# Shared expert in units of 256 rows, its first layer split around its second; B turned by four transposes

## The chip, the cores and the metric

The kernel runs on one core of one Trainium2 chip. A core has PE (matrix products, with its weight loads), DVE (vector), ACT (scalar functions and copies), POOL (general) and SP (which here issues most transfers). Each engine works through its own list of instructions in order, and waits where an operand or a buffer is not there yet. The metric is the device time of one launch in microseconds (us); lower is better.

## The reference, cut to what matters

Four sequences of 1024 tokens with 256 channels go through a Mamba block, a layer norm, a mixture of experts and a second layer norm.

```python
# Mamba block: 512 inner channels, 16 states
h = rms_norm(x) @ w_in                         # 256 -> 1024, split into xs and res
xs = silu(causal_conv4(xs)); res = silu(res)
delta_low, B, C = split(xs @ w_xproj, [16, 32])
delta = softplus(delta_low @ w_dt + b_dt)
state[l] = exp(delta * A) * state[l-1] + delta * xs * B[l]    # per channel and state
y = sum_n(state * C);  x = layernorm(x + x + ((y + xs * D) * res) @ w_out)
# mixture of experts: 8 routed experts, 2 for each token, and one shared by all
normed = rms_norm(x)
shared = relu(normed @ sw1 + sb1) @ sw2 + sb2                 # 256 -> 1024 -> 256
w, idx = top2(sigmoid(normed @ router_w.T)), weights normalised
routed = sum over the 2 chosen e of w_e * (relu(normed @ ew1[e] + eb1[e]) @ ew2[e] + eb2[e])
x = layernorm(x + shared + routed)
```

All of it is in float32.

## The kernel before

**Chunks and scan.** The 4096 tokens are 8 chunks of 512, two for each sequence. A chunk's scan has 16 steps, one for each state `n`. A step handles four blocks of 128 channels: ACT makes `da` (an exponential of 128x512, L515), DVE runs the recurrence (L518), multiplies by the row of C (L531) and, for the next step, multiplies `xs` by the row of B (L451). POOL does the fourth block of that product (L456) and adds each step's result into `y` (L532). The rows of B and C are spread over partitions by small products on PE, `pb` (L437). In the first chunk, steps from 3 on get their input from PE instead, by products with a diagonal matrix (`diagonal`, `products`), which need B with tokens on partitions: `B_T`.

**Front.** `front` makes the inputs of a chunk's scan. Its projection `pp` (L360) holds the low rank of delta, then B, B and C in quads of 32 partitions. In the first chunk B with tokens on partitions is computed a second time at this place, by 16 products (`B_T`, L368) that take blocks of `xs` as weights. ACT copies 16 rows of `pp` into `proj` (L377), and `pz` (L393) makes delta of it; softplus follows with an exponential, a logarithm `y<-y` (L417), an add on POOL (`delta`, L421), and ACT then starts `y` with `xs * D` (L424). The first chunk's front runs alone; the others run beside the scan of the chunk before.

**Experts.** `tail` finishes a chunk: output projection, layer norm, routing, and the scatter of token rows to the lists of their experts (POOL, L707). It also leaves `x1T`, the normed rows with channels on partitions, and `combT`. The work of the experts is then a list of units of 128 rows: for each chunk 4 units of the shared expert and, in the chunks' order, 1, 11, 8, 8, 8, 8, 8 and 16 routed blocks. `up` is a unit's first layer: two halves of eight products `pu` of 128 columns each in one PSUM buffer of the pool `ps_up` (two buffers), and four evictions by ACT with bias and ReLU into a buffer `h` of 128x4x128 (L911). `down` is the second layer: eight products of 256 columns into `pd` (pool `ps_dn`, one buffer). For the shared expert a ninth adds the biases (L939), and ACT copies `pd` into one half of `rs` (pool `one`, a single buffer, L947); after every second unit POOL issues a transfer that adds `rs` to `sums` in memory (L952). For routed blocks ACT scales into `rb` and an indirect transfer adds it (L964).

`moe` orders a unit: weights ahead (`need`), the first layer of the next unit, the transposes of the rows of the unit after that (`rows_T`, `pbt`), then the second layer of this unit, then the rows of later blocks (`load_rows`). Each `yield` is one step. Weights of the first and of the second layer have two buffers each; all shared units of a chunk use one load.

**What sets the order.** The loop over scan steps calls `other_work` four times a step, which owes 0.85 of an expert step each time. On top of that a planner in the framework orders each engine's list when the kernel is built, by its own estimate of when operands are ready; buffers of a pool are handed out in the order of the program's text. After the last scan the rest of the expert units run with the last chunk's `tail`, and `finish` normalises and writes the output.

Of the kernel before, what the change touches and what calls it, by code (L numbers as in the profile page):

```python
# [8 lines left out]
F32 = mybir.dt.float32  # L9
# [4 lines left out]
P = 128  # L14
# [28 lines left out]
BS = P  # L43
TOKENS = NSEQ * SEQ
# [26 lines left out]
def mamba_moe_kernel(  # L71
# [189 lines left out]
    def front(b, c):  # L261
# [101 lines left out]
        if alone:  # L363

            pt = ps_up.tile([P, TC // P, N], F32, tag="up", name="B_T")
            for t in range(TC // P):
                for k in range(KB):
                    nc.tensor.matmul(  # L368
                        pt[:, t, :], lhsT=xs[:, k, t * P : (t + 1) * P], rhs=w_xp_sb[:, k, QUAD : QUAD + N],
                        start=(k == 0), stop=(k == KB - 1),  # L370
                    )
            by_token.append(pt)
# [3 lines left out]
        proj = one.tile([R, TC], F32, tag="proj", name=f"proj_{s}")  # L376
        nc.scalar.copy(proj, pp[0:R, :])  # L377
# [85 lines left out]
    def turned():  # L463

        xs, TT = scans[chunks[0]][0], LEN[chunks[0]] // P
        pt = by_token.pop()
        B_T = const.tile([P, TT, N], F32, tag="B_T", name="B_T_sb")
        nc.scalar.copy(B_T, pt)
        x_T = two.tile([P, TT, DI], F32, tag="w2", name="x_T")
        by_token.extend((x_T, B_T))  # L470
        for k in range(KB):
            pt = ps_up.tile([P, TT, P], F32, tag="up", name=f"x_T_{k}")
            for t in range(TT):
                nc.tensor.transpose(pt[:, t, :], xs[:, k, t * P : (t + 1) * P], ident)
            nc.scalar.copy(x_T[:, :, k * P : (k + 1) * P], pt)
            if k % 2:
                yield
# [65 lines left out]
    def tail(b, c):  # L543
# [52 lines left out]
        shared_left.extend(range(TC // BS))  # L596
# [203 lines left out]
    for b, c in chunks:  # L800
        units += [(b, c, SHARED, j) for j in range(LEN[b, c] // BS)]
        units += [(b, c, None, j) for j in range(BLOCKS[b, c])]
# [65 lines left out]
    def rows_T(u):  # L868
# [4 lines left out]
        if e is not None:  # L873
            rows_in[u] = channels[b, c][0][:, :, j * BS : (j + 1) * BS]
            return
# [15 lines left out]

    def up(u, hidden):
# [3 lines left out]
        wb = held[key(u)]["b"]  # L896
        for h in range(2):
# [24 lines left out]
    shared_rows, pending = {}, []  # L922

    def down(u, hidden):
# [3 lines left out]
        for h in range(2):  # L928
            for i in range(half):
# [3 lines left out]
                    start=(m == 0), stop=(m == HB - 1 and e is None),  # L933
# [3 lines left out]
        if e is not None:  # L937

            nc.tensor.matmul(  # L939
                pd, lhsT=channels[b, c][1][:, j * BS : (j + 1) * BS], rhs=b2_sb,  # L940
                start=False, stop=True,
            )
            shared_left.pop()
            if j % 2 == 0:
                shared_rows[b, c] = one.tile([P, 2, D], F32, tag="rs", name=f"rs_{u}")
            rs = shared_rows[b, c]
            nc.scalar.copy(rs[:, j % 2, :], pd)  # L947
            if j % 2:
                first = P + b * SEQ + FIRST[b, c] + (j - 1) * BS

                def add():
                    nc.gpsimd.dma_start(  # L952
                        sums_of[first : first + 2 * BS, :].rearrange("(t p) d -> p t d", p=P),
                        rs, accum_op=ALU.add,
                    )

                pending.append(add)
            return
# [13 lines left out]
    def moe():  # L972

        hidden = {}
        for u in range(last):
# [8 lines left out]
            for v in range(u + 1, u + 3):  # L984
                need(v, "w1")
            if u + 1 < last and ready(u + 1):
                hidden[u + 1] = []
                for _ in up(u + 1, hidden[u + 1]):
                    yield True
            evict_all()  # L990
            need(u + 3, "w1")
# [5 lines left out]
            for _ in down(u, hidden.pop(u)):  # L997
                yield True
# [209 lines left out]
```

## Time and profile before

| | |
|---|---|
| time, median of 3 runs | 1596.62 us (1595.63 to 1603.1) |
| the profiled execution: time; span of its instructions | 1597.39 us; 1595.7 us |
| busy: PE, DVE, POOL, ACT | 1256.2, 1279.3, 1140.0, 1065.6 us |
| `da` exponentials on ACT, 512 | 353.0 us, 697 ns each |
| recurrences on DVE after `da`, idle before them for `da` | 47.7 us in 22 places |
| first layer of shared units: 1024 PE instructions | 133.2 us busy |
| evictions of all first layers on ACT, 800 | 229.2 us, 368 ns each |
| `rs` copies on ACT, 32 | 11.8 us, 369 ns each; 14.7 us of waiting for the add in 4 places |
| `B_T` products, 32 PE instructions | 6.5 us busy |

A line of the page or of an answer gives source line, engine and operation, then output and inputs by the program's names. In lists in order of time the first two numbers are the start and the duration in us, and the bracket is the idle time before and what ended it. PE counts a float32 product as two instructions. Busy shares are means over stages with different limits.

### The profile page before, as it was taken

The numbers are of one execution on the slowest core, as the hardware profiler recorded it, in microseconds if no ns is written. First come the engines' busy times: TensorE is split into PE (matmuls) and PEld (weight loads), VectorE is DVE, ScalarE is ACT, GpSimd is POOL, SyncE is SP. The second block draws the span as 40 slices with busy tenths as digits, with TensorE's granted clock in tenths as the row PEclk, the third lists the DMA queues.
The fourth block names the chain that finished last, engine by engine and source line by source line (L and its number), as shares of the span: only waits on it lengthen the run. The fifth ranks groups of instructions, "written<-read, shape, count | busy, mean of one in ns | idle before, by whom it ended". The sixth has DMA issues, their size and how long they took to land. (4 is left out here: it accounts for less than half of the span.)

```text
span 1595.7 us, 20861 instructions
## 1 busy us (share of the span) xinstructions
PE 1256.2 (79%) x6667; PEld 971.3 (61%) x6667; DVE 1279.3 (80%) x1422; ACT 1065.6 (67%) x2345; POOL 1140.0 (71%) x886
## 2 busy tenths in 40 slices
PE   6588366874678798979798879888779978999990
PEld 3356233652356666667567756776567767889980
DVE  3899899989997798989998999999989889320005
ACT  4757557775778567877788778766786757434442
POOL 2378975898678876898689978987799787431123
PEclk8699777977789999999998999899999999999995
DMA  4000000441016552475246633564167448559986
GB/s 121 1 0 1 26 14 14 149 116 20 13 61 182 173 173 77 141 213 179 54 123 194 194 85 121 171 185 106 51 191 208 129 126 248 166 160 323 308 269 218
DMA packets 160276, 211.65 MB, mean 133 GB/s; under 512 B 20617, under 2 KB 138130, under 8 KB 160162
## 3 DMA queue, kind: packets, MB, share of 16 engines
q1 hardware_dynamic: 135954, 181.75, 35.1%
q0 software_dynamic: 17216, 21.57, 7.6%
q10 hardware_dynamic: 6992, 6.95, 1.3%
q8 instruction: 55, 0.90, 0.2%
q14 instruction: 59, 0.48, 0.1%
HBM read 178.97 MB, written 31.27 MB: 132 GB/s over the span
## 5 line engine op out<-in xcount | busy, mean ns | idle before, releaser
L532 POOL TENSOR_TENSOR y<-y,hs 128x2048 f32<-128x2048 f32 x128 | 595.8, 4655 | 82.1 <-DVE hs L531 81.7
L515 ACT ACTIVATE da<-delta,chan_sb 128x512 f32<-128x512 f32 x512 | 353.0, 697 | 196.6 <-DVE hs L518 191.6
L931 PE MATMUL pd<-w,h 128*128 128x256 f32 x1600 | 390.6, 389 | 24.6 <-ACT h L911 11.3
L931 PEld LDWEIGHTS pd<-w,h 128*128 128x128 f32 x1600 | 301.8, 195 | 95.1 <-issue 20.0
L518 DVE TENSOR_TENSOR_SCAN hs<-da,state,hs 128x512 f32<-128x512 f32 x256 | 317.8, 1270 | 27.8 <-ACT da L515 26.7
L902 PEld LDWEIGHTS pu<-xT,w 128*128 128x128 f32 x2176 | 275.5, 203 | 61.2 <-ACT xT L885 42.1
L902 PE MATMUL pu<-xT,w 128*128 128x128 f32 x2176 | 280.3, 287 | 28.2 <-ACT xT L885 28.2
L531 DVE TENSOR_TENSOR hs<-hs,pb 128x2048 f32<-128x2048 f32 x128 | 290.8, 2272 | 2.3 <-ACT state L526 0.8
L911 ACT ACTIVATE h<-pu,wb 128x128 f32<-128x128 f32 x800 | 229.2, 368 | 69.8 <-PE pu L902 65.5
L518 DVE TENSOR_TENSOR_SCAN hs<-da,hs 128x512 f32<-128x512 f32 x204 | 240.9, 1209 | 20.9 <-ACT da L515 20.5
L456 POOL TENSOR_TENSOR hs<-xs,b 128x512 f32<-128x512 f32 x118 | 169.4, 1439 | 68.0 <-ACT b L449 49.1
L451 DVE TENSOR_TENSOR hs<-xs,pb 128x1536 f32<-128x1536 f32 (+1 forms) x115 | 198.0, 1722 | 13.3 <-ACT b L449 7.7
L964 POOL DMA_INDIRECT sums<-rb,xb x68 | 107.9, 1587 | 133.3 <-ACT rb L961 33.5
L293 PE MATMUL pi<-hT,w_in_sb 128*128 128x512 f32 x256 | 142.8, 683 | 32.8 <-DVE xs L325 12.3
L437 PE MATMUL pb<-parts,pick 128*128 128x512 bf16 x243 | 97.3, 403 | 76.0 <-DVE hs L451 26.0
L219 DVE BATCH_NORM_STATS2 bnst_l<-o 128x6 f32<-128x256 f32 x32 | 11.9, 410 | 156.2 <-DMA o<-sums 156.2
L902 PEld LDWEIGHTS pu<-x1T,w 128*128 128x128 f32 x1024 | 127.8, 199 | 14.3 <-issue 10.3
L902 PE MATMUL pu<-x1T,w 128*128 128x128 f32 x1024 | 133.2, 285 | 0.0
L293 PEld LDWEIGHTS pi<-hT,w_in_sb 128*128 128x128 f32 x256 | 50.4, 214 | 98.4 <-issue 34.8
L564 PE MATMUL po<-w_out_sb,y 128*128 128x256 f32 x256 | 68.7, 429 | 34.7 <-POOL y L554 28.7
L564 PEld LDWEIGHTS po<-w_out_sb,y 128*128 128x128 f32 x256 | 54.4, 218 | 54.0 <-POOL y L554 35.7
L707 POOL DMA_INDIRECT rows<-hn,to x64 | 63.2, 987 | 33.0 <-issue 15.8
(198 smaller groups left out, 1562.0 us busy)
## 6 DMA issues: line engine op xcount, KB each, us to landing
w<-in_ew SPq DMA_DIRECT2D x136, 1024.0 KB
w<-in_sw SPq DMA_DIRECT2D x16, 1024.0 KB
xb<-rows SPq DMA_DIRECT2D x68, 129.0 KB
x<-in_x SPq DMA_DIRECT2D x8, 512.0 KB
sums<-summed ACTq DMA_DIRECT2D x8, 512.0 KB
sums<-rs POOLq DMA_DIRECT2D x16, 256.0 KB
o<-sums SPq DMA_DIRECT2D x3, 1024.0 KB
out<-o ACTq DMA_DIRECT2D x3, 640.0 KB
```

Of the source, the lines that this page charges most:

```text
L293: nc.tensor.matmul(pi, lhsT=w_in_sb[:, k, m * P : (m + 1) * P], rhs=hT[:, k, :], start=(k == 0), stop=(k == KD - 1),)
L451: nc.vector.tensor_tensor(hs[:, 0:on_pool, :], xs[:, 0:on_pool, :], pb.unsqueeze(1).to_broadcast([P, on_pool, TC]), ALU.mult,)
L456: nc.gpsimd.tensor_tensor(hs[:, k, :], xs[:, k, :], copy, ALU.mult)
L515: nc.scalar.activation(da, delta[:, k, :], AF.Exp, scale=chan_sb[:, k, CA + n : CA + n + 1])
L518: nc.vector.tensor_tensor_scan(hs[:, k, :], da, scaled_inputs.pop(0) if by_pe(step) else hs[:, k, :], 0.0 if c == 0 else state[:, k, n : n ...
L531: nc.vector.tensor_tensor(hs, hs, pb.unsqueeze(1).to_broadcast([P, KB, LEN[b, c]]), ALU.mult)
L532: nc.gpsimd.tensor_tensor(y, y, hs, ALU.add)
L564: ins = nc.tensor.matmul(po[:, i, :], lhsT=y[:, k, t * P : (t + 1) * P], rhs=w_out_sb[:, k, :], start=(k == 0), stop=(k == KB - 1),)
L902: nc.tensor.matmul(pu[:, i, :], lhsT=w[:, k, at : at + P], rhs=xT[:, k, :], start=(k == 0), stop=(k == KD - 1),)
L911: nc.scalar.activation(t[:, i, :], pu[:, i, :], AF.Relu, bias=wb[:, m : m + 1])
L931: nc.tensor.matmul(pd, lhsT=hidden[h][:, i, :], rhs=w[:, m, :], start=(m == 0), stop=(m == HB - 1 and e is None),)
L964: nc.gpsimd.indirect_dma_start(sums_of[:, :], bass.IndirectOffsetOnAxis(xb[:, TOKEN : TOKEN + 1].bitcast(U32), 0), rb, None, compute_op=AL ...
```

## The change

`front` no longer computes B a second time. It copies 64 rows of `pp` in place of 16 for the first chunk, and `turned` makes `B_T` by four transposes of that copy.

The shared expert works in units of 256 rows, two for each chunk. Its first layer is made in quarters: `quarter` issues four products of 256 columns into one PSUM buffer, and two evictions of 128x256. `up` does two quarters of such a unit; `down_shared` does the second layer in four quarters, with the third and fourth quarter of its own first layer after its first two, and the two first steps of the next unit's `up` ahead of its last two. `pd` is 128x2x256, and one copy moves it to `rs`. In `moe` the weights after next are asked for inside `down_shared`. `down` keeps the routed part alone. Routed units are otherwise as before.

```diff
+PAIR = 2 * BS
@@ front @@
-        if alone:
-            pt = ps_up.tile([P, TC // P, N], F32, tag="up", name="B_T")
-            for t in range(TC // P):
-                for k in range(KB):
-                    nc.tensor.matmul(
-                        pt[:, t, :], lhsT=xs[:, k, t * P : (t + 1) * P], rhs=w_xp_sb[:, k, QUAD : QUAD + N],
-                        start=(k == 0), stop=(k == KB - 1),
-                    )
-            by_token.append(pt)
...
-        proj = one.tile([R, TC], F32, tag="proj", name=f"proj_{s}")
-        nc.scalar.copy(proj, pp[0:R, :])
+        low_rank = one.tile([2 * QUAD if alone else R, TC], F32, tag="proj", name=f"proj_{s}")
+        nc.scalar.copy(low_rank, pp[0 : low_rank.shape[0], :])
+        proj = low_rank[0:R, :]
+        if alone:
+            by_token.append(low_rank)
@@ turned @@
+        pt = ps_up.tile([P, TT, 2 * QUAD], F32, tag="up", name="low_rank_T")
+        for t in range(TT):
+            nc.tensor.transpose(
+                pt[:, t, :], low_rank[:, t * P : (t + 1) * P], ident[0 : 2 * QUAD, 0 : 2 * QUAD]
+            )
...
-        nc.scalar.copy(B_T, pt)
+        nc.scalar.copy(B_T, pt[:, :, QUAD : QUAD + N])
@@ tail @@
-        shared_left.extend(range(TC // BS))
+        shared_left.extend(range(TC // PAIR))
@@ units, rows_T @@
-        units += [(b, c, SHARED, j) for j in range(LEN[b, c] // BS)]
+        units += [(b, c, SHARED, j) for j in range(LEN[b, c] // PAIR)]
...
-            rows_in[u] = channels[b, c][0][:, :, j * BS : (j + 1) * BS]
+            rows_in[u] = channels[b, c][0][:, :, j * PAIR : (j + 1) * PAIR]
+    def quarter(u, q, xT, hidden):
+        w, wb = held[key(u)]["w1"], held[key(u)]["b"]
+        pu = ps_up.tile([P, 2, PAIR], F32, tag="up", name=f"pu_{u}_{q}")
+        for i in range(2):
+            for k in range(KD):
+                at = (2 * q + i) * P
+                nc.tensor.matmul(
+                    pu[:, i, :], lhsT=w[:, k, at : at + P], rhs=xT[:, k, :],
+                    start=(k == 0), stop=(k == KD - 1),
+                )
+        def evict():
+            t = hid.tile([P, 2, PAIR], F32, tag="h", name=f"h_{u}_{q}")
+            for i in range(2):
+                m = 2 * q + i
+                nc.scalar.activation(t[:, i, :], pu[:, i, :], AF.Relu, bias=wb[:, m : m + 1])
+            hidden.append(t)
+        evictions.append(evict)
@@ up @@
+        if units[u][2] is not None:
+            for q in range(2):
+                quarter(u, q, xT, hidden)
+                yield
+                evict_all()
+            hidden.append(xT)
+            return
+    def down_shared(u, hidden, ahead):
+        b, c, e, j = units[u]
+        w, xT = need(u, "w2"), hidden.pop()
+        pd = ps_dn.tile([P, 2, D], F32, tag="dn", name=f"pd_{u}")
+        for q in range(4):
+            if q >= 2:
+                next(ahead, None)
+                yield
+                evict_all()
+            for i in range(2):
+                m = 2 * q + i
+                for t in range(2):
+                    nc.tensor.matmul(
+                        pd[:, t, :], lhsT=hidden[q][:, i, t * P : (t + 1) * P], rhs=w[:, m, :],
+                        start=(m == t == 0), stop=False,
+                    )
+            if q == 3:
+                for t in range(2):
+                    at = j * PAIR + t * P
+                    nc.tensor.matmul(
+                        pd[:, t, :], lhsT=channels[b, c][1][:, at : at + P], rhs=b2_sb,
+                        start=False, stop=(t == 1),
+                    )
+            yield
+            evict_all()
+            if q < 2:
+                quarter(u, q + 2, xT, hidden)
+                yield
+                evict_all()
+            if q == 1:
+                need(u + 2, "w1")
+        for _ in ahead:
+            pass
+        shared_left.pop()
+        rs = one.tile([P, 2, D], F32, tag="rs", name=f"rs_{u}")
+        nc.scalar.copy(rs, pd)
...
@@ moe @@
-            for v in range(u + 1, u + 3):
-                need(v, "w1")
+            routed = units[u][2] is None
+            need(u + 1, "w1")
+            if routed:
+                need(u + 2, "w1")
+            ahead = iter(())
             if u + 1 < last and ready(u + 1):
                 hidden[u + 1] = []
-                for _ in up(u + 1, hidden[u + 1]):
+                ahead = up(u + 1, hidden[u + 1])
+            if routed:
+                for _ in ahead:
                     yield True
-            evict_all()
-            need(u + 3, "w1")
+                evict_all()
+                need(u + 3, "w1")
...
-            for _ in down(u, hidden.pop(u)):
+            of = hidden.pop(u)
+            for _ in down(u, of) if routed else down_shared(u, of, ahead):
                 yield True
```

More of the change, by code (lines that the diff above doesn't have):

```diff
@@ L465, in turned @@
         xs, TT = scans[chunks[0]][0], LEN[chunks[0]] // P
-        pt = by_token.pop()
+        low_rank = by_token.pop()
+        pt = ps_up.tile([P, TT, 2 * QUAD], F32, tag="up", name="low_rank_T")
[3 more added lines that the diff above has]
+            )
         B_T = const.tile([P, TT, N], F32, tag="B_T", name="B_T_sb")
-        nc.scalar.copy(B_T, pt)
+        nc.scalar.copy(B_T, pt[:, :, QUAD : QUAD + N])
         x_T = two.tile([P, TT, DI], F32, tag="w2", name="x_T")
@@ L920, in evict_all, with add @@
             evictions.pop(0)()
-    shared_rows, pending = {}, []
+    pending = []
+    def down_shared(u, hidden, ahead):
[34 more added lines that the diff above has]
+        nc.scalar.copy(rs, pd)
+        first = P + b * SEQ + FIRST[b, c] + j * PAIR
+        def add():
+            nc.gpsimd.dma_start(
+                sums_of[first : first + PAIR, :].rearrange("(t p) d -> p t d", p=P),
+                rs, accum_op=ALU.add,
+            )
+        pending.append(add)
     def down(u, hidden):
@@ L932, in down @@
                     pd, lhsT=hidden[h][:, i, :], rhs=w[:, m, :],
-                    start=(m == 0), stop=(m == HB - 1 and e is None),
+                    start=(m == 0), stop=(m == HB - 1),
                 )
@@ L936, in down @@
             evict_all()
[L937 to L958, printed above, removed]
         xb = blocks_in.pop(u)
```

## The prediction

> **What bounds the kernel now.** I read three things, in this order: the share of busy time by stage, the waits of the engine that is nearest to full, and the stretches in which that engine does nothing. The first view is the busy time of each engine in chosen stretches (columns after the bounds: length, then busy us of PE, weight load, DVE, ACT, POOL; then the granted clock, the DMA share and GB/s).
>
> ```profile
> 40.00:80.00 40.00, 22.18 (x75) 12.99 (x73) 35.84 (x41) 30.84 (x48) 15.23 (x9) 0.62 0.00 1
> ...
> 800.00:1200.00 400.00, 338.51 (x1813) 261.86 (x1814) 377.82 (x393) 312.33 (x695) 342.60 (x228) 0.95 0.48 142
> ...
> 1440.00:1480.00 40.00, 40.00 (x274) 37.14 (x274) 0.00 (x0) 16.83 (x56) 7.49 (x5) 1.00 1.01 321
> ```
>
> So there are three stages: a start of some 57 us in which the first chunk's steps follow each other, then the scan until about 1360 us, where DVE is busy 94% of the time in the stretch shown, then a closing stretch to 1556 us that belongs to PE (40.00 of 40.00), and 40 us of final output. A saving counts at the start if it is on the chain, in the scan if it feeds DVE sooner, and at the close if it shortens PE.
>
> The chain of waits at the start, in order of time:
>
> ```profile
> 30.16 6.00 PE L368 MATMUL B_T<-w_xp_sb,xs 128*128 128x16 f32 x28
> 30.40 0.57 ACT L377 COPY proj<-pp 16x512 f32<-16x512 f32 x1 [1.94 <-PE pp L360]
> ...
> 36.08 7.19 PE L393 MATMUL pz<-proj,w_dt_sb 16*128 16x512 f32 x8
> 36.19 0.21 ACT L468 COPY B_T_sb<-B_T 128x64 f32<-128x64 f32 x1 [4.74 <-PE B_T L368]
> ```
>
> `proj` is ready at 30.97, but `pz`, which everything after needs, starts at 36.08: PE is doing the small B products.
>
> In the scan, the instructions in order of time show what DVE's largest gaps stand behind. In three chunks it is this pair:
>
> ```profile
> 314.51 0.37 ACT L947 COPY rs<-pd 128x256 f32<-128x256 f32 x1 [4.53 <-DMA sums<-rs]
> 315.51 2.47 DVE L518 TENSOR_TENSOR_SCAN hs<-da,state,hs 128x512 f32<-128x512 f32 x2 [3.26 <-ACT da L515]
> ...
> 490.08 0.37 ACT L947 COPY rs<-pd 128x256 f32<-128x256 f32 x1 [4.97 <-DMA sums<-rs]
> 491.15 1.22 DVE L518 TENSOR_TENSOR_SCAN hs<-da,hs 128x512 f32<-128x512 f32 x1 [4.78 <-ACT da L515]
> ```
>
> ACT works in order. The third unit's copy into the single `rs` buffer waits for the add of the first two units to read it, and the exponentials `da` behind it come late. The third place is 1310.44 (ACT waits 4.82) and 1317.20 (DVE waits 4.99). DVE loses 3.26 + 4.78 + 4.99 = 13.0 us.
>
> Other gaps stand where ACT has the last pieces of the next chunk's front:
>
> ```profile
> 331.90 2.56 ACT L424 ACTIVATE y<-xs,chan_sb 128x512 f32<-128x512 f32 x4 [3.47 <-POOL delta L421]
> 335.58 2.46 DVE L518 TENSOR_TENSOR_SCAN hs<-da,state,hs 128x512 f32<-128x512 f32 x2 [5.26 <-ACT da L515]
> ```
>
> **The start.** Out go 32 products of 16 columns, of which 28 take the 6.00 us above. In come 4 transposes of the 64-row copy of `pp`; in the built order they stand just ahead of `pz`. The nearest row is the transposes of `x_T`, 8 in 1.97 us, so 4 take 1.0. The copy has 64 rows in place of 16; a 128-row copy of the same `pp` takes 0.57 like the 16-row one, so nothing is added. `pz` starts at 30.97 + 0.1 + 1.0 = 32.1, that is 3.9 us sooner, and all up to the first scan hangs on it. Bounds: -5 (no transposes on the path) and -3 (each takes the 0.43 us that is their mean in the trace).
>
> **The scan: `rs`.** One copy of 128x512 per 256 rows replaces two of 128x256, and between two of them now lie eight steps of expert work in place of four. In the built order of chunk 1 the add of the first stands on POOL three long adds (4.66 us each) ahead of the second's own add, so it should have landed. I take the 13.0 us as gone; at worst half returns.
>
> **The scan: cheaper evictions.** Per 256 rows 16 evictions of 128x128 become 8 of 128x256. In a row 4 of the former take 1.14 us, 0.285 each; for the latter the nearest row is `rb<-pd` (128x256, 468 ns alone, so about 0.39 in a row). That is 4.56 against 3.12 us, 1.4 us by 14 units in the scan, 20 us of ACT. ACT idles 192 us for DVE anyway: I count nothing.
>
> **The scan: what is moved.** A shared unit now carries half of its own first layer and the next unit's, and the built order shows the consequence. The rows of the second routed block are transposed ahead of the shared unit's third quarter, and the first routed block's rows are asked for only after the weights of the second, on SP; those weights wait for the fourth quarter. So around scan steps 10 to 12 PE has little expert work, and at steps 13 to 15 both routed blocks come together. On ACT their evictions then stand ahead of a `da`, in six chunks: eight of them (2.3 us) between the second and third `da` of step 13 or 14, where none or four stood. These are the gaps just shown, where DVE already waits. Part is covered by the wait for POOL (3.47 us in chunk 1, 0.76 to 1.38 in the next five), and in chunks 1 and 5 an eviction group leaves the earlier gap. Chunk by chunk I get +0.6, +1.5, +0.5, +1.5, +0.3, +1.5, about +6 us. Bounds: 0 (all hidden) and 36 (2.3 us, plus 3.7 us waiting for 32 products of a routed block, in six chunks). The broadcasts `pb` behind the bundle on PE were let past while PE was free, so I count no wait for them.
>
> **The close.** Two rules of the Trainium skill bear on it. The row first: a 128-row unit's first layer is 32 instructions in 3.73 us, or 117 ns each; 16 instructions of 256 columns (`pd`) take 3.62, or 226. "TensorE: Matmul & The Clock Gate", Back-to-back issue gap, gives paired weight loads and matmuls 81 ns at 128 columns and 131 at 512, so doubling the columns would cost far less than double: by an estimate between these, 98 ns at 256, 40% off the first layer, 6 us in the last chunk's four units. By the row it is 0.11 us a unit, 0.4 us. I take the row (fp32, this kernel).
>
> The second rule speaks against the change, through the stop at the first routed block:
>
> ```profile
> 1424.59 0.35 SPq L858 DMA_DIRECT2D xb<-rows  x1
> ...
> 1427.89 0.41 PE L881 MATMUL pbt<-ident,xb 128*128 128x128 f32 x2 [2.97 <-DMA xb<-rows]
> ...
> 1428.13 5.31 PE L931 MATMUL pd<-w,h 128*128 128x256 f32 x16
> ...
> 1433.99 3.84 PE L902 MATMUL pu<-xT,w 128*128 128x128 f32 x32
> ```
>
> Same work, 5.31 us after a stop of 3 us against 3.62 elsewhere: 1.7 us of slow clock. Before, the next unit's first layer starts 14.2 us after those rows land (1442.06). After the change PE reaches this point at about the same time (one 3.7 us first layer less, three quarters of a 4.2 us second layer and a 0.9 us wait for the `rs` copy more). Then, from the landing: transposes 0.4, ten products of 256 columns to the end of the fourth quarter 4.5, slow clock 1.7: 6.6. Weights and rows are issued (1.0) and rows land 3.3 us later as above (1424.59 to 1427.89): 10.9, or 14.2 if they queue behind the 1 MB of weights at the 321 GB/s of this stretch; I take 12.5. Nothing covers the rest: transposes and eviction 1.1 us, then 3.73 us of first layer: 17.4. So +3.2 us, and 1 us more because 2 MB of weights now load beside the scatter whose end the rows wait for. The second stop is under 2 us; the page's Why this matters for your kernels counts stops above about 3 us, so I add no slow clock, where a like stop by the row would cost another 1.7. Together +4; bounds 0 and +8.
>
> **Sum:** -3.9 - 13.0 + 6 - 0.4 + 4 = -7.3 us. The profiled execution took 1597.39 (span 1595.7 and 1.7 around it), 0.8 above the median of 1596.62: 1590.1 on its scale, **1589.5 us** on the median's.
>
> **Rivals.** (1) The bundles at steps 13 to 15 are hidden, and nothing else changes: 6 us less, 1583. For it: PE and ACT have slack there; against: DVE already waits at just these places. (2) Slower: each of the six bundles keeps DVE waiting, because the evictions, in order on ACT, wait for the products and `da` waits for them. It decides at 13.3 / 6 = 2.2 us a chunk, where the gain is used up; at 4.2 us a chunk the time is 1597 + 25 - 13 = 1609. For it: 5.26, 3.06 and 3.11 us gaps there now. (3) The `rs` wait is replaced, not removed: the second shared unit's first product directly follows the first's last in the only `pd` buffer, so PE waits for an ACT copy in every chunk, and the following evictions and `da` with it. Then -3.9 + 6 + 4 - 0.4, about 1602.
>
> **How the numbers follow.** Forecast 0.40 (own range 1584 to 1596), rival 1 0.21, rival 2 0.27, rival 3 0.12. 0.5% is 8 us, about what can be told from no change. Faster: 0.16 of the forecast and rival 1. Same: 0.24 of it, 0.08 of rival 3, 0.03 of rival 2. Slower: the rest. Below 1577 all bounds would have to fall well, 0.05; above 1610 lies half of rival 2. The range is 1577 to 1610.
>
> **What would show it.** `pz` starts near 32; `rs` waits for no DMA; DVE's gaps before `da` at steps 13 and 14 grow by 1 to 2 us in chunks 1 to 6; the closing stretch has two stops, about 5 and 2 us, and a slow second layer after the first. It is wrong if the `da` gaps grow by over 2.2 us a chunk, if the time from the last `pb` to the final block changes by more than 8 us, or if DVE's waits for `da` don't fall from 47.7 us.

## The result

The change makes the kernel slower: 1617.53 us (median of 4 runs, 1613.85 to 1619.31) against 1596.12 us for the kernel before beside it (4 runs, 1590.68 to 1603.1). The ratio is 1.0144, with a 95% interval from 1.0117 to 1.0171. The prediction was 1589.5 us with a range to 1610. The profiled execution took 1617.48 us, its span is 1615.8 us, 20.1 more than before.

The busy time by stage of the changed kernel (columns as in the prediction):

```profile
800.00:1200.00 400.00, 341.26 (x1609) 254.45 (x1608) 367.32 (x380) 297.72 (x624) 335.10 (x222) 0.92 0.47 140
1440.00:1480.00 40.00, 36.04 (x217) 32.38 (x218) 0.00 (x0) 14.88 (x49) 4.39 (x3) 0.91 0.72 217
```

The stages are as before, but two are less full. In the scan DVE works 367.32 us of 400 in place of 377.82. In the close PE, which set the time there with 40.00 of 40.00, has a hole of 4 us, and its granted clock is 0.91 in place of 1.00.

To see where the 20 us arise, four marks are enough: the start of the last output product (`hs<-hs,pb`) of the first chunk and of the last chunk, the start of the last run of `pd` products, and the end. Chunks and scan steps are counted from 0.

| stretch | before | after | difference | predicted |
|---|---|---|---|---|
| start and first chunk, to its last output product | 182.44 | 178.00 | -4.4 | -3.9 |
| scan of the other seven chunks, to 1361.84 and 1366.45 | 1179.40 | 1188.45 | +9.0 | -7.0 |
| close, to the last `pd` run at 1551.62 and 1569.45 | 189.78 | 203.00 | +13.2 | +3.6 |
| final output | 44.1 | 46.4 | +2.3 | 0 |

The edit has no part in the final output; its 2.3 us are not explained here (with e9 below it took 42.8).

The start's gain is near the prediction. In order of time, TensorE at the start:

```profile
28.92 3.43 PE L361 MATMUL pp<-xs,w_xp_sb 128*128 128x512 f32 x4 [2.73 <-ACT xs L330]
33.01 0.46 PE L463 MATMUL low_rank_T<-ident,proj 64*128 64x64 f32 x4 [0.67 <-ACT proj L368]
33.41 1.98 PE L387 MATMUL pz<-proj,w_dt_sb 16*128 16x512 f32 x4
```

The four transposes take 0.46 us, and `pz` follows them at once, 1.0 us after the copy of `pp` began. It starts at 33.41 and not at 32.1 because `pp` itself came later in this execution: its copy starts at 32.38, before at 30.40.

What the prediction said of `rs` also holds in itself. The view of all instructions that touch `rs`: what ACT and POOL sat idle for before them.

```profile
L990 ACT COPY rs<-pd x16: 574/580/635, 295.1 to 1454.7; 128x512 f32<-128x512 f32 x16
...
  ACT rs L990: 24.7, 2
  issue: 3.7, 1
  PE pd L974: 3.4, 3
```

There is no line for the transfer `sums<-rs`, where before 14.7 us in 4 places stood. Yet DVE's waits for `da` did not fall:

```profile
DVE hs L517 <- ACT da L514: 48.2, 22, 6.7
```

Before, it was 47.7 us in 22 places. So other waits of the same kind took the place of those removed.

**Where the close lost.** The list of TensorE in order of time, first in the last chunk's scan, then in the close. `pu<-x1T,w` and `pd` at L966 are the shared units, here a chunk's second, `pbt` is the transposes of routed rows, `pb` belongs to the scan.

```profile
1306.39 3.77 PE L966 MATMUL pd<-w,h 128*128 128x256 f32 x12
1310.03 0.38 PE L431 MATMUL pb<-parts,pick 128*128 128x512 bf16 x1
1314.47 0.61 PE L431 MATMUL pb<-parts,pick 128*128 128x512 bf16 x2 [4.07 <-DVE hs L445]
1319.20 0.59 PE L431 MATMUL pb<-parts,pick 128*128 128x512 bf16 x1 [4.13 <-DVE hs L530]
1323.22 0.61 PE L431 MATMUL pb<-parts,pick 128*128 128x512 bf16 x1 [3.43 <-DVE hs L445]
1323.63 0.64 PE L880 MATMUL pbt<-ident,xb 128*128 128x128 f32 x2
1324.05 6.03 PE L898 MATMUL pu<-x1T,w 128*128 128x256 f32 x16
...
1434.44 2.86 PE L966 MATMUL pd<-w,h 128*128 128x256 f32 x12 [0.68 <-ACT rs L990]
1442.51 0.69 PE L880 MATMUL pbt<-ident,xb 128*128 128x128 f32 x2 [5.21 <-DMA xb<-rows]
1442.99 3.62 PE L898 MATMUL pu<-x1T,w 128*128 128x256 f32 x8
1446.40 1.91 PE L966 MATMUL pd<-w,h 128*128 128x256 f32 x4
...
1455.65 0.45 PE L880 MATMUL pbt<-ident,xb 128*128 128x128 f32 x2 [1.00 <-DMA xb<-rows]
1456.55 5.66 PE L930 MATMUL pu<-xT,w 128*128 128x128 f32 x48 [0.46 <-ACT xT L884]
```

Both places show the same thing. The transposes of the second routed block stand inside the second shared unit, ahead of half its first layer and at least half its second. That work runs as soon as the transposes are through, but TensorE takes its list in order, so it waits until the routed rows have landed. In the close the stop is 5.21 us and shows as such. In the last chunk's scan it is a stretch of 13 us, from 1310.2 to 1323.6, that the view of waits hides: short `pb` products of the scan run in it, so the idle time is put down to DVE, and the expert work that stands still appears nowhere. The kernel before has a stop of its own at this place, half as long. It is the wait for `rs`, which held TensorE too, and not the transposes, which ran ahead of it:

```profile
1302.40 0.38 PE L881 MATMUL pbt<-ident,xb 128*128 128x128 f32 x2
...
1310.86 1.22 PE L931 MATMUL pd<-w,h 128*128 128x256 f32 x2 [6.17 <-ACT rs L947]
```

So the change took one stop of TensorE away here and put in a longer one.

SP's queue over the same places tells why the rows are late:

```profile
1312.73 1.00 SPq L842 DMA_DIRECT2D w<-in_ew  x2
1314.94 1.48 SPq L857 DMA_DIRECT2D xb<-rows  x2
...
1430.58 1.03 SPq L842 DMA_DIRECT2D w<-in_ew  x2
1440.09 1.48 SPq L857 DMA_DIRECT2D xb<-rows  x2
```

In both places 2 MB of weights are issued first, then the rows. In the last scan chunk the block list (`plan`, on DVE) is ready at 1311.5 and the first transposes run at 1323.63, 12.1 us later; before, these marks are 1298.47 and 1302.40, 3.9 us apart. In the close the last scatter on POOL is issued at 1433.63 and the rows 6.5 us after it; before, at 1421.95 and 2.6 us.

One number joins the two places. Count the `pu` and `pd` instructions that start after a point of time on TensorE (64 of 128 columns, or half as many of 256, are one block of 128 rows). When the output product of step 7 of the last chunk starts, 29.9 blocks are left before and 29.8 after. At step 10 it is 27.3 and 29.0, and at the end of the scan 23.4 and 24.5. The last scan chunk has no chunk behind it in which the lag can be made up: 1.1 blocks, at 7.25 us from one to the next in the close, are some 8 us more work for it. TensorE's idle time between the two marks of the close grew from 6.7 to 12.1 us, by 5.4. Together that is about the 13.2 us.

**Where the scan lost.** Up to the end of chunk 2 the lead over before grew from 4.4 to 9.1 us. Chunks 3 to 6, which had no `rs` wait before, then lost 15.1 us, where 3.8 had been forecast for them, and the last chunk won 1.5. The predicted sort of loss is there. ACT and DVE at step 13 of chunk 5 (ACT in the first fence, DVE in the second):

```profile
1013.59 0.72 ACT L418 ACTIVATE y<-xs,chan_sb 128x512 f32<-128x512 f32 x1 [1.19 <-POOL delta L415]
1014.22 1.12 ACT L939 ACTIVATE h<-pu,wb 128x128 f32<-128x128 f32 x4
1015.22 1.95 ACT L418 ACTIVATE y<-xs,chan_sb 128x512 f32<-128x512 f32 x3
1017.06 1.15 ACT L939 ACTIVATE h<-pu,wb 128x128 f32<-128x128 f32 x4
1018.05 1.34 ACT L514 ACTIVATE da<-delta,chan_sb 128x512 f32<-128x512 f32 x2
```

```profile
1018.82 2.46 DVE L517 TENSOR_TENSOR_SCAN hs<-da,state,hs 128x512 f32<-128x512 f32 x2 [5.04 <-ACT da L514]
```

Eight evictions of routed blocks stand ahead of `da`, and DVE waits 5.04 us where it waited 3.11. But there is another sort of place that the prediction did not have. ACT at step 2 of chunk 4:

```profile
723.77 0.47 ACT L1016 ACTIVATE rb<-pd,xb 128x256 f32<-128x256 f32 x1 [4.57 <-PE pd L1008]
724.14 0.58 ACT L443 COPY b<-pb 128x512 f32<-128x512 f32 x1
725.77 1.14 ACT L939 ACTIVATE h<-pu,wb 128x128 f32<-128x128 f32 x4 [1.05 <-PE pu L930]
726.78 0.71 ACT L514 ACTIVATE da<-delta,chan_sb 128x512 f32<-128x512 f32 x1
```

ACT's copy of a routed result (`rb`) waits 4.57 us for its `pd`, which stands on TensorE behind the output projection `po`. The `da` behind it comes late, and DVE waits 2.15 us (and 1.12 for `po`). Before, half of that `pd` ran ahead of `po`, and the same copy followed the exponentials without a wait at this point. The `po` itself, before and after:

```profile
719.45 3.72 PE L564 MATMUL po<-w_out_sb,y 128*128 128x256 f32 x16 [0.20 <-POOL y L554]
...
717.46 5.41 PE L563 MATMUL po<-w_out_sb,y 128*128 128x256 f32 x16 [3.49 <-POOL y L553]
```

The same 16 instructions take 1.7 us longer where TensorE stood still for 3.49 us ahead of them. ACT's waits for routed `pd` grew from 54.0 to 76.5 us in all. Not all of this is a loss: of the 5.4 us that DVE waits at step 2 of chunks 4 and 6, 3.1 come back at step 4, where a wait for `b` is gone.

### The profile page after: what moved, and what is told of

Read it like the earlier page. It is cut to its first block, busy times and chain, and to the rows that moved or that the text cites. A ratio compares the mean times of both kernels' runs of the same rounds, so it can differ in the third digit from the quotient of the medians.

```text
span 1615.8 us, 19638 instructions
## 1 busy us (share of the span) xinstructions
PE 1268.8 (79%) x6127; PEld 959.3 (59%) x6127; DVE 1278.1 (79%) x1422; ACT 1044.5 (65%) x2201; POOL 1139.4 (71%) x886
## 5 line engine op out<-in xcount | busy, mean ns | idle before, releaser
L930 PEld LDWEIGHTS pu<-xT,w 128*128 128x128 f32 x2176 | 267.9, 199 | 38.4 <-ACT xT L884 16.0
L930 PE MATMUL pu<-xT,w 128*128 128x128 f32 x2176 | 272.0, 283 | 20.1 <-ACT xT L884 9.9
L1008 PE MATMUL pd<-w,h 128*128 128x256 f32 x1088 | 259.8, 385 | 11.7 <-ACT rb L1016 7.9
L1008 PEld LDWEIGHTS pd<-w,h 128*128 128x128 f32 x1088 | 204.0, 193 | 51.5 <-ACT rb L1016 12.0
L450 POOL TENSOR_TENSOR hs<-xs,b 128x512 f32<-128x512 f32 x118 | 171.9, 1466 | 63.0 <-ACT b L443 46.0
L939 ACT ACTIVATE h<-pu,wb 128x128 f32<-128x128 f32 x544 | 155.3, 371 | 51.4 <-PE pu L930 47.7
L966 PE MATMUL pd<-w,h 128*128 128x256 f32 x512 | 142.2, 420 | 15.5 <-ACT rs L990 8.0
L966 PEld LDWEIGHTS pd<-w,h 128*128 128x128 f32 x512 | 106.3, 211 | 59.8 <-ACT rs L990 16.7
L898 PE MATMUL pu<-x1T,w 128*128 128x256 f32 x512 | 133.6, 404 | 0.0
L898 PEld LDWEIGHTS pu<-x1T,w 128*128 128x128 f32 x512 | 102.6, 205 | 27.3 <-issue 12.1
L563 PE MATMUL po<-w_out_sb,y 128*128 128x256 f32 x256 | 76.8, 465 | 44.6 <-POOL y L553 37.3
```

The source lines that it names most:

```text
L450: nc.gpsimd.tensor_tensor(hs[:, k, :], xs[:, k, :], copy, ALU.mult)
L898: nc.tensor.matmul(pu[:, i, :], lhsT=w[:, k, at : at + P], rhs=xT[:, k, :], start=(k == 0), stop=(k == KD - 1),)
L930: nc.tensor.matmul(pu[:, i, :], lhsT=w[:, k, at : at + P], rhs=xT[:, k, :], start=(k == 0), stop=(k == KD - 1),)
L939: nc.scalar.activation(t[:, i, :], pu[:, i, :], AF.Relu, bias=wb[:, m : m + 1])
L966: nc.tensor.matmul(pd[:, t, :], lhsT=hidden[q][:, i, t * P : (t + 1) * P], rhs=w[:, m, :], start=(m == t == 0), stop=False,)
L1008: nc.tensor.matmul(pd, lhsT=hidden[h][:, i, :], rhs=w[:, m, :], start=(m == 0), stop=(m == HB - 1),)
```

## The experiments

Each kernel is given as the ratio of its time to that of the kernel before beside it, with a 95% interval, and the span of its profiled execution (1595.7 before, 1615.8 after).

| kernel | ratio | interval | span |
|---|---|---|---|
| the change | 1.0144 | 1.0117 to 1.0171 | 1615.8 |
| before + new B (e1) | 0.9964 | 0.9941 to 0.9988 | 1588.2 |
| changed, rows asked for at a unit's start (e4) | 1.0109 | 1.0066 to 1.0151 | 1605.5 |
| changed, last chunk as before (e5) | 1.0083 | 1.0056 to 1.0110 | 1608.1 |
| before + new B, last chunk changed (e6) | 1.0010 | 0.9994 to 1.0027 | 1593.0 |
| changed, routed transposes behind and rows first (e9) | 0.9988 | 0.9970 to 1.0006 | 1590.3 |
| as e9, units not interleaved (e7) | 0.9985 | 0.9973 to 0.9997 | 1600.5 |
| before + new B + small `rs` buffers (e3) | 0.9910 | 0.9881 to 0.9940 | 1581.7 |
| before + new B + paired `pd` (e8) | 0.9899 | 0.9875 to 0.9923 | 1584.6 |
| as e8, first routed blocks held back (e10) | 0.9950 | 0.9929 to 0.9971 | 1584.2 |
| changed, routed transposes behind only (e11) | 1.0117 | 1.0087 to 1.0147 | 1618.0 |
| changed, rows first only (e12) | 1.0141 | 1.0107 to 1.0175 | 1614.8 |
| as e9, 128 columns again (e13) | 0.9982 | 0.9961 to 1.0002 | 1587.1 |

### The new B alone

The edit is the diff of `front` and `turned` applied to the kernel before, and nothing else.

> The kernel before with only the new B: 64 rows of the projection copied and turned by four transposes, no second computation of B. Theory S (the start's gain is whole and is kept): 4.3 us less than before, about 1592, and every milestone of the scan earlier by 4.3 to 4.5 us. Rival (it is taken back by a later wait, in the scan or at the close): within 1 us of before.

Measured 0.9964, that is 5.7 us less with an interval from 1.9 to 9.4. In the trace the first output product starts at 60.50 in place of 65.63, 5.1 us sooner, and every mark to the end of the scan keeps between 3.6 and 7.4 us of lead. Theory S holds: the start's saving is real and kept.

### Which stage loses: the last chunk against the others

A function says which chunks use units of 256 rows; both forms of `up` and `down` are in the kernel. In e5 the last chunk has the former units and the seven others the new ones; in e6 it is the other way round.

```diff
+def paired(b, c):
+    return (b, c) != (NSEQ - 1, 1)        # e5; e6 has == here
...
-        units += [(b, c, SHARED, j) for j in range(LEN[b, c] // PAIR)]
+        units += [(b, c, SHARED, j) for j in range(LEN[b, c] // (PAIR if paired(b, c) else BS))]
...
-            routed = units[u][2] is None
+            routed = not is_pair(u)
```

> The changed kernel with the last chunk's shared expert in the former units of 128 rows; the seven other chunks as changed. Theory A and B alike (two thirds of the loss arise in the scan): 8 us of the scan stay and the close is as before, 1605 to 1609. Rival C (the close loses most): 1597 or less.

> The kernel before with the new B and with the last chunk alone in units of 256 rows. Theory A and B: minus 4.3 for the start, plus 7 for the close (5.2 us stop instead of 3.0, first routed block 3.3 us later after its rows, 1 to 2 us of scatter beside weights), so 1598 to 1600. Rival C: 1605 or more.

e5 measured 1.0083, which at 1596 us is 1609; e6 measured 1.0010, 1598. Both are where theories A and B had them, and rival C (the close loses most) falls. The scan of the last chunk runs beside the shared units of the chunk before it, so the stretch of 13 us belongs to e5 (24.5 blocks left at the end of the scan) and not to e6 (23.4). Against e1, the last chunk's new units alone cost 0.0046, 7.3 us (the forecast for this term was +4, bounds 0 and 8). The seven other chunks cost 0.0119 against e1, 19 us, although they hold the gain from `rs`.

### Rows in the order of the units: an experiment that missed its aim

```diff
             routed = units[u][2] is None
+            if not routed:
+                load_rows(u + 1)
+                load_rows(u + 2)
             need(u + 1, "w1")
             if routed:
                 need(u + 2, "w1")
+            else:
+                rows_T(u + 1)
...
-            rows_T(u + 2)
+            if routed:
+                rows_T(u + 2)
...
             need(u + 2, "w2")
+            rows_T(u + 2)
```

> The changed kernel, but a shared unit asks for the rows of the next two routed blocks at its start, the first block's rows are transposed before the second's, and the second's only after the unit's second layer. Theory A (the loss of the scan comes from the two first routed blocks being held up and coming together, and that of the close from the first block's rows being asked for last): 4 us back at the close and 8 to 14 in the scan, so 1600 to 1606. Rival B (the scan's loss comes from how the half-size pieces of shared work and the last pieces of the next chunk's front stand to each other on ACT and POOL, whatever the routed blocks do): only the close's 4 us, about 1613.

Measured 1.0109, 1613 us: the value of rival B. But the trace shows that the edit did not do what it was made for. In the close SP issued the weights at 1424.36 and the first rows at 1433.70, 6.0 us after the last scatter's issue at 1427.68, hardly less than the 6.5 of the changed kernel. At the start of the first shared unit the block list is not there yet, and by the second the weights are already on the queue. The first routed transposes, still inside the second shared unit, stopped TensorE for 4.64 us in the close. So it is no evidence against the late rows.

### Transposes behind the shared unit and rows before weights

Nothing of a routed block stands inside a shared unit any more, and the rows are asked for just ahead of the weights. The step of `down_shared` that belongs to the next unit is left out where that unit has none to give.

```diff
@@ down_shared @@
             if q >= 2:
-                next(ahead, None)
-                yield
+                if next(ahead, "none") is None:
+                    yield
                 evict_all()
...
             if q == 1:
+                load_rows(u + 1)
+                load_rows(u + 2)
                 need(u + 2, "w1")
@@ moe @@
+            if not routed:
+                load_rows(u + 1)
+                load_rows(u + 2)
             need(u + 1, "w1")
...
-            if u + 1 < last and ready(u + 1):
+            if u + 1 < last and ready(u + 1) and (routed or units[u + 1][2] is not None):
...
-            rows_T(u + 2)
+            if routed:
+                rows_T(u + 2)
...
+            if not routed:
+                rows_T(u + 1)
+                load_rows(u + 2)
             need(u + 2, "w2")
```

> The changed kernel with the transposes of the first two routed blocks moved behind the second layer of the second shared unit (nothing of a routed block stands inside a shared unit), their rows asked for before the weights, and no step given away where the next unit has nothing to do. Theory D (TensorE works in order, and the second routed block's transposes inside the last shared unit keep three quarters of that unit waiting for rows that land late: a 13 us hole in the last scan chunk leaves a unit more for the close, and the close has a 5.2 us stop): 6 us back at the close and 7 from the unit, up to 8 more in the scan, so 1.000 to 1.006 times before, 1596 to 1605. Theory E (half-size pieces and 256-row evictions between the exponentials cost the scan by themselves): 1.010 or more, 1611 and up, since the scan's loss stays.

Measured 0.9988 (0.9970 to 1.0006): 25 us less than the changed kernel, at the favourable end of what theory D gave. TensorE's list at the two places:

```profile
1305.65 2.32 PE L966 MATMUL pd<-w,h 128*128 128x256 f32 x10
1308.58 0.59 PE L431 MATMUL pb<-parts,pick 128*128 128x512 bf16 x2 [0.61 <-DVE hs L445]
1309.01 1.46 PE L966 MATMUL pd<-w,h 128*128 128x256 f32 x6
1310.40 1.12 PE L974 MATMUL pd<-b_sb,combT 9*128 9x256 f32 x4
1311.45 0.44 PE L880 MATMUL pbt<-ident,xb 128*128 128x128 f32 x2
...
1426.52 3.62 PE L966 MATMUL pd<-w,h 128*128 128x256 f32 x16
1430.07 1.13 PE L974 MATMUL pd<-b_sb,combT 9*128 9x256 f32 x4
1431.12 0.44 PE L880 MATMUL pbt<-ident,xb 128*128 128x128 f32 x2
1432.18 2.09 PE L930 MATMUL pu<-xT,w 128*128 128x128 f32 x16 [0.62 <-ACT xT L884]
```

The shared unit runs through, and neither place has a stop for rows. 23.5 blocks are left at the end of the scan, 23.4 before. From the last output product to the last `pd` run it takes 188.6 us (203.0 in the changed kernel, 189.8 before): 14.4 us of the gain lie there. The scan of the seven chunks takes 1180.9 us in place of 1188.45, another 7.6, and ACT's waits for routed `pd` are 47.0 us. But of the 15.1 us that chunks 3 to 6 lost, 10.4 are still lost in e9. The order of transposes and rows explains the close and the last chunk, and only a smaller part of the scan.

### The interleaving itself

As the last kernel, but `up` of a 256-row unit makes all four quarters, `down_shared` all four of its own, and no other unit's work stands between; `moe` asks for the weights after next at a unit's start again.

```diff
-            for q in range(2):
+            for q in range(4):
                 quarter(u, q, xT, hidden)
                 yield
                 evict_all()
-            hidden.append(xT)
             return
...
-            if q < 2:
-                quarter(u, q + 2, xT, hidden)
-                yield
-                evict_all()
```

> As the last, but a shared unit of 256 rows makes its whole first layer, then its whole second, with nothing of another unit between. Theory D: within 0.3% of the last one, since the interleaving was not what cost. Theory E: at least 8 us less than the last one.

Measured 0.9985 against 0.9988: the same. Theory E, that half-size pieces between the exponentials cost by themselves, falls; and splitting the layers brought no gain that can be told.

### Each half of the mending alone

e11 is e9 without the early `load_rows` calls: transposes behind, rows still behind the weights. e12 is the changed kernel with only these calls ahead of the weights (in `down_shared`, and one for the first block after the first shared unit): rows first, transposes still inside.

```diff
@@ e12, down_shared and moe @@
             if q == 1:
+                load_rows(u + 1)
+                load_rows(u + 2)
                 need(u + 2, "w1")
...
+            if not routed:
+                load_rows(u + 2)
             need(u + 2, "w2")
```

> The changed kernel with nothing of a routed block inside a shared unit, as in the kernel that took 0.9988 times before, but with rows and weights asked for where the changed kernel asks for them. Theory D (the place of the transposes on TensorE decides): within 4 us of that kernel, 0.998 to 1.001 times before. Rival F (the rows asked for late on the queue decide): more than half of the 25 us loss is back, 1.006 or more.

> The changed kernel with one thing altered: the rows of the first routed block (and of the second, where its list is known) are asked for on SP's queue before the weights of that block; the transposes stay inside the last shared unit. Theory F (rows behind 2 MB of weights decide: in the changed kernel the issue of the rows came 6.5 us after the last scatter's, with rows first 2.7): the scatter's delay of 3.7 us and most of the hole in the last chunk are gone, 0.999 to 1.004 times before. Theory D+F (both are needed, since the transposes moved alone brought nothing back): 1.006 or more, because the second block's rows still stand behind the weights and its transposes stop the last shared unit.

e11 measured 1.0117 and e12 1.0141. Neither half alone brings back more than some 4 of the 25 us, and with intervals that overlap the changed kernel's it may be nothing; theory D alone falls, theory F alone falls, and D+F holds. The traces show how each half is undone. In e11 the rows of the later blocks and four weights go out ahead of the first block's rows, and TensorE stops behind the shared unit instead of within it:

```profile
1436.68 1.12 PE L974 MATMUL pd<-b_sb,combT 9*128 9x256 f32 x4
1450.57 0.69 PE L880 MATMUL pbt<-ident,xb 128*128 128x128 f32 x2 [12.77 <-DMA xb<-rows]
1451.72 6.55 PE L930 MATMUL pu<-xT,w 128*128 128x128 f32 x32 [0.46 <-ACT xT L884]
```

In e12 SP's queue has the first block's rows first, as wanted, 2.7 us after the last scatter at 1433.54:

```profile
1436.26 0.35 SPq L857 DMA_DIRECT2D xb<-rows  x1
...
1437.36 0.95 SPq L842 DMA_DIRECT2D w<-in_ew  x2
1438.49 1.57 SPq L857 DMA_DIRECT2D xb<-rows  x2
```

But TensorE's first routed transposes are those of the second block, whose rows are the next to go and land 8.0 us after their issue, behind the 2 MB of weights:

```profile
1434.22 3.72 PE L966 MATMUL pd<-w,h 128*128 128x256 f32 x16 [0.68 <-ACT rs L992]
1446.48 0.69 PE L880 MATMUL pbt<-ident,xb 128*128 128x128 f32 x2 [8.53 <-DMA xb<-rows]
```

The time from the block list to the first routed transposes in the last scan chunk sorts the kernels too: 3.9 us before, 12.1 in the changed kernel, 12.2 in e12, 22.4 in e11, 5.8 in e9. Those with more than 12 have 24.2 to 24.5 blocks left at the end of the scan, the two others 23.4 and 23.5.

### What the wait for `rs` was worth

Two ways to take the wait out of the kernel before, both with the new B. e3 gives each unit of 128 rows its own copy and its own add, with two buffers of half the size. e8 lets two units write into one PSUM bank and copies once.

```diff
@@ e3, down @@
-            if j % 2 == 0:
-                shared_rows[b, c] = one.tile([P, 2, D], F32, tag="rs", name=f"rs_{u}")
-            rs = shared_rows[b, c]
-            nc.scalar.copy(rs[:, j % 2, :], pd)
+            rs = one.tile([P, D], F32, tag="rs", name=f"rs_{u}", bufs=2)
+            nc.scalar.copy(rs, pd)
...
@@ e8, down @@
+            if j % 2 == 0:
+                shared_rows[b, c] = ps_dn.tile([P, 2, D], F32, tag="dn", name=f"pd_{u}")
+            pd = shared_rows[b, c][:, j % 2, :]
...
             if j % 2:
+                rs = one.tile([P, 2, D], F32, tag="rs", name=f"rs_{u}")
+                nc.scalar.copy(rs, shared_rows[b, c])
```

> The kernel before with the new B and, alone of the expert work, two buffers of 128 rows for the copy of the shared expert's result in place of one of 256, with one add each (four adds a chunk in place of two). Theory R (the copy's wait for the add cost 13 us in chunks 1, 2 and 7 and is gained whole): 0.988 times before, 1577. Rival R2 (the waits come back in front of other exponentials; the changed kernel's waits for them fell by only 3.4, 1.9 and 2.4 us in those chunks): 0.991 to 0.997, so 1582 to 1590.

> The kernel before with the new B and with the second layers of two shared units of 128 rows in one PSUM bank and one copy for both, after the second; units, order and adds as before. Theory R: as the last kernel, 0.988. Rival R2: 0.991 to 0.997. If the halved number of copies matters for itself (16 copies of 0.58 us in place of 32 of 0.37), 2 to 3 us less than the last kernel.

Measured 0.9910 and 0.9899. In neither does `rs` wait for a transfer, and DVE's waits for `da` fall to 41.1 and 39.6 us. Against e1 (0.9964) the wait was worth 8.6 and 10.4 us, between rival R2's lower values and theory R's 13: most of it is gained, a part comes back ahead of other exponentials. The halved number of copies makes no difference beyond the intervals. e8 has the lowest ratio of this study, though not apart from e3: 1% faster than before and 2.4% faster than the change (0.9899 / 1.0144).

### What is left between e9 and e8

e9 has the same copies as e8 but is 0.9% slower, 14 us. e10 adds to e8 that the first two routed blocks of a chunk stand behind the shared units; e13 gives e9's products 128 columns and its evictions 128x128 again.

```diff
@@ e10, moe @@
+            shared = units[u][2] is not None
-            if u + 1 < last and ready(u + 1):
+            if u + 1 < last and ready(u + 1) and not (shared and units[u + 1][2] is None):
...
-            rows_T(u + 2)
+            if not shared:
+                rows_T(u + 2)
...
+            if shared:
+                rows_T(u + 1)
@@ e13, quarter @@
-                    pu[:, i, :], lhsT=w[:, k, at : at + P], rhs=xT[:, k, :],
+                    pu[:, i, r], lhsT=w[:, k, at : at + P], rhs=xT[:, k, r],
...
-                nc.scalar.activation(t[:, i, :], pu[:, i, :], AF.Relu, bias=wb[:, m : m + 1])
+                    nc.scalar.activation(t[:, i, r], pu[:, i, r], AF.Relu, bias=wb[:, m : m + 1])
```

> The kernel before with the new B and with two second layers in one PSUM bank and one copy (0.990 times before), and in addition the first two routed blocks of a chunk held back: neither their transposes nor the first one's first layer stand ahead of the second layer of the last two shared units. Theory H (what the scan of chunks 1 to 6 still loses in the changed kernel and its mended forms, some 9 us against shared units of 128 rows, comes from the first routed blocks standing later in the lists, whatever the width of a shared unit): 8 to 10 us of it appear here, 0.995 to 0.997 times before. Theory W (it comes from the units of 256 rows): 0.989 to 0.992, no loss in chunks 1 to 6.

> The mended form that took 0.9988 times before (units of 256 rows, rows before weights, nothing routed inside a shared unit), with the products of the first layer of 128 columns and its evictions of 128x128 again, in the same order. Theory W1 (the 256-row width of products and evictions is what still costs the scan 9 us in chunks 1 to 6): 6 to 9 us back, 0.993 to 0.995. Theory W2 (the order of the larger units costs it, and the width is no loss): 0.998 or more, with 1 to 3 us on top for 16 more evictions a unit.

e13 measured 0.9982, the same as e9 within the intervals, so theory W1 falls at its size, 6 to 9 us. A smaller cost of the width is not excluded: eight of e13's twelve executions took 1587.8 to 1591.3 us and four 1595.4 to 1599.5, and in its trace, which is one of the eight, chunks 3 to 6 lose 5.6 us where e9 loses 10.4. e10 measured 0.9950, 8 us more than e8, which is the size that theory H named. But H placed it in the scan of chunks 1 to 6, and there the traces show 0.6 us of it, 1.7 in the whole scan; the span of that profiled execution is no longer than e8's. So holding the blocks back costs in the timed runs, where it costs is not settled, and some 6 us between e10 and e9 stay without a proven cause.

One difference was not tested. The mean granted clock of an execution is 0.90 at the median in every kernel whose first seven chunks have units of 128 rows (before, e1, e3, e6, e8, e10), 0.88 to 0.89 in every one with 256 rows there (the change, e4, e5, e7, e9, e11, e12), and 0.894 in e13. In the traces, chunks 3 to 6 lose between nothing and 4.1 us in the first group and 8.6 to 18.5 in the second. Whether the lower clock costs part of this, or only mirrors the stops of TensorE, no run here separates.

## Why the prediction was wrong

**The start (-3.9)** was right within what can be told: -4.4 in the changed kernel, -5.1 in the trace of e1 and -5.7 in its time (interval -1.9 to -9.4). Two of the prediction's sums are off in the last digits, without effect: 36.08 - 32.1 is 4.0, and 1596.62 - 7.3 is 1589.3.

**`rs` (-13.0)** was right in kind: no copy waits for the add any more, in the changed kernel as in e3 and e8. Measured alone it is 8.6 and 10.4 us. Rival 3 also has its grain: TensorE does wait for the ACT copy at the unit boundary (8.0 us before `pd` in five places), but that does not carry the loss.

**Cheaper evictions** were sized right: first-layer evictions fell from 229.2 us to 155.3 + 53.4 = 208.7, 20.5 us, and as the prediction had it, nothing is seen to come of it (e13, with the former evictions, is not slower than e9). A 256-row form takes 467 ns where two of 128 take 2 x 371.

**The scan, what is moved (+6)** is the step that failed. The waits it priced are there: at steps 11 to 14 of chunks 1 to 6 DVE's waits for `da`, apart from the two behind `rs`, changed by -1.0, +1.0, +1.5, +0.9, +2.9 and +1.4 us, together 6.7. What it left out follows from the sentence ahead of the price: "around scan steps 10 to 12 PE has little expert work". It gave that a consequence on ACT and put the one on TensorE at nothing. Two things followed. The lag of the last scan chunk cannot be made up and came out as 1.1 blocks, some 8 us, in the close; e9, which mends the order, has it no more. And in chunks 3 to 6, where 3.8 us were forecast, 15.1 came. Of these 6.7 stand at steps 11 to 14, and the rest at places the step didn't look at: at step 2 of the chunk after, where `rb` waits for `pd` behind `po` (5.4 us in chunks 4 and 6, 2.3 with what came back), and at step 10, where POOL's share of the next input comes late (`hs` at L450, 1.5, 0.5 and 2.2 us in chunks 4 to 6). What causes these is read from the trace and not shown: e9 still loses 10.4 us in the same chunks.

Of the prediction's three signs of being wrong one came: DVE's waits for `da` did not fall (48.2 us against 47.7). The `da` gaps grew by 1.1 us a chunk and not by 2.2. The time from the last `pb` to the final block grew by only 1.4 us, because the last `pb` of the scan came later as well; that sign could not see the lag.

**The close (+4)** had the right mechanism. From the landing of the second block's rows to the boundary between the two routed first layers (1456.55 plus 3.73) it is 17.8 us where the prediction had 17.4. The second stop, 1.00 us and 0.46, brought no slow clock, as taken: the 48 instructions after it take 118 ns each. The term that was mis-sized is "1 us more because 2 MB of weights now load beside the scatter": the rows are issued 6.3 to 6.5 us after the last scatter's issue in the changed kernel, e6 and e11, and 2.6 to 2.8 us in the kernels with rows first, before, e5, e7, e9 and e12. That is 3.7 us more in place of 1 and makes the term 6.7, near the 7.3 of e6 against e1. The price of columns was right: the shared first layer is busy for 133.6 us with half the instructions (133.2 before), so the page's cheaper long rows ("TensorE: Matmul & The Clock Gate", Back-to-back issue gap, in the Trainium skill) do not appear in this fp32 kernel.

**The rivals.** The time lies above the slower rival's 1609, and its mechanism (evictions that keep DVE waiting in each chunk) did not decide: its places cost 6.7 us, not 25. The case that came, an order on TensorE that no longer fits the order of the loads, was in none of them, though both halves stood in the text: SP's order in the scan's step, TensorE's stop in the close's.

## What to carry to other kernels

An engine with slack can still lose time for good: if work that is ready stands in its list behind an instruction that waits for a load, ask not only who waits for its results but whether the lag can be made up before the list ends: here the last chunk had nothing behind it. When a step is moved, compare its place in the engine's list with the place of its load in the queue: either mended alone brought back at most some 4 us of 25. And ask for small loads that something waits for ahead of large ones that nothing waits for yet.

## What was not expected of the hardware

A pair of 1 MB weight loads issued during the last indirect scatter held back the scatter's end: rows that wait for it were issued 6.0 to 6.5 us after its last issue in four kernels (the change, e4, e6, e11) and 2.6 to 3.5 us in the ten others. SP's longest wait for the scatter's transfer there is 6.5 us in the changed kernel and 3.1 in e12, which differs by the loads' order. A further 129 KB load behind such a pair landed 8.0 us after its issue (e12), where one without it took 3.3 us before.

The very first part of the program, the same in all kernels with the new B, reached its first output product between 58.3 and 63.2 us in the profiled executions. A difference of 3 us between two single profiles is therefore no evidence by itself; marks were compared from the end of the first chunk on, and verdicts taken from the ratios.
